# A graph network on one Trainium2 core: the order of a square's small transfers, its store and its subtractions

## The chip, the cores and the metric

The kernel runs on one core of a Trainium2 chip. The metric is the device time of one execution in microseconds (us), as a median over runs. Three runs of the kernel before took 11475.05, 11484.36 and 11488.69 us.

A core has a matrix engine (PE), a vector engine (DVE), a scalar engine for activations (ACT), a general one (POOL) and a queue that here only issues transfers (SP). Each works through its own instructions in order, and they wait for one another by semaphores. Transfers between DRAM and the on-chip memory are issued by SP or POOL and carried out by 16 DMA engines.

## The reference

Four layers on a graph of N = 3327 nodes with 128 features and a dense 3327 x 3327 matrix `adj`. Only the first layer matters here: attention with D = 128 heads of H = 8 elements, in which `adj` is added twice to the scores.

```python
q = (x @ Wq.T).reshape(d, n, h)
k = (x @ Wk.T).reshape(d, n, h)
v = (x @ Wv.T).reshape(d, n, h)
a = jnp.einsum('dnh,dmh->dnm', q, k) * scale
a = a + spatial_encoding + edge_encoding      # both are adj
a = jax.nn.softmax(a, axis=2)
out = jnp.einsum('dnm,dmh->dnh', a, v)
out = out.reshape(n, h * d)
return out @ Wo.T
```

The other three layers multiply features by `adj` or its transpose and come after the attention.

## The kernel before, in words

The kernel computes transposed scores: for a chunk `c` of 476 queries (7 chunks), a group `g` of 4 heads (32 groups) and a pair `q` of key tiles (13 pairs), so 7 x 32 x 13 = 2912 pairs. The sum starts in a PSUM bank with the transposed `adj` tile (`seed`, L660, on DVE), PE adds the products of keys and queries (`scores`, L666), ACT takes the exponential (`exps`, L678 and L681; in three pairs of a group a part of it is done on DVE by a polynomial, L692 to L703), and PE sums values with it (`values`, L719). At a group's end DVE copies the sums (`OS`, L727) and POOL sends them out in four transfers (L731).

The order is written by hand. The loop at L790 goes through slots, four to a pair, and everything is emitted in that order; each engine keeps it. What a pair emits besides its own work is:

- `loads` (L733): at the second pair of each group SP issues the next group's load: 16 transfers of keys (`KT`, L564), 24 of queries (`QS`, L566 and L568) and one of values (`VR`, L581), 41 in all. At the fifth pair POOL negates queries (L576), lays out values (`VA`, L586) and with a small copy (`seen`, L590) waits for all of them; PE's first product of the next group waits for `seen`.
- whatever `plan` has put down for the pair (L803 to L805), emitted ahead of that pair's `loads`.

`plan_squares` (L761) plans the squares. A square is a strip of 128 rows of `adj` which has to be transposed into columns (`cols`, 128 partitions x 26 tiles x 128) for the next chunk, and from which a bound for each row's scores must be subtracted so that the exponential stays in range. The first 4 of the 26 squares are done before the attention; the other 22 are spread over chunks 0 to 5, each starting in group 7k + 1 of its chunk. A square goes through these steps:

1. Four quarters, one in each of four groups: `load` (SP), `turn` (two transposes on DVE) and `largest` (a row maximum on DVE, L297, into `rm`). The last `largest` comes one pair before the pair called U below.
2. `store` (L300, SP): 1664 KB from `cols` to `adjT`, in pieces of 512 bytes. The later layers read it, and chunk 0 and a bit of chunk 1.
3. `gather` (L312, SP): four transfers of 512 bytes each from `rm` to `rowmax_d` in DRAM, element by element: 4 x 128 writes of four bytes.
4. `back` (L317, SP): `four`, the same maxima read again with the rows on the partitions.
5. `finish` (DVE, L321 and L322, then SP, L323): the maximum of the four, plus a bound of the products, and its write to `bound_d`, 128 writes of four bytes.
6. `spread` (L304, SP): the bounds read to all partitions (`on_all`), 64 KB. SP has to wait for the landing of `bound_d` before it issues this.
7. `shift` (L307, POOL): 13 subtractions of `on_all` from two tiles of `cols` each, in place. They need `on_all`, and the store from `cols` must be over.
8. `store` again, to `adjS`, which the next chunk's loads (L604) read in its predecessor's last group.

`cols`, `rows` and `on_all` have one buffer each, so the next square's first transpose waits for the store to `adjS`.

Of the kernel before, what the change touches and what calls it, by code (L numbers as in the profile page):

```python
# [29 lines left out]
NQ = NT // 2  # L30
# [55 lines left out]
def squares_of(c):  # L86

    return 0 if c < 0 else -(-min(CW * (c + 1), NP) // P)
# [3 lines left out]
def gnn_kernel(ctx: ExitStack, tc: tile.TileContext, x, adj, Wq, Wk, Wv, Wo, embed, layer,  # L92
# [12 lines left out]
    shifted_by_tile = adjS.rearrange("(p t) n -> t p n", t=NT)  # L105
# [233 lines left out]
    with tc.tile_pool(name="a1", bufs=1) as a1, tc.tile_pool(name="a2", bufs=2) as a2, \  # L339
# [23 lines left out]
        for t0 in range(0, NT, 2):  # L363
            for s in "kq":
# [3 lines left out]
                for i in range(2):  # L368
                    t = t0 + i
                    sq = a4.tile([P, H, P], F32, name="sq")  # L370
# [167 lines left out]
    with tc.tile_pool(name="e1", bufs=1) as e1, tc.tile_pool(name="e_adj", bufs=30) as e_adj, \  # L538
# [76 lines left out]
        with tc.If(loose < 1), tc.manual_schedule():  # L615
# [117 lines left out]
            def loads(u):  # L733

                c, g, q = pairs[u]
                k = c * NG + g
                if k + 1 < NC * NG:
                    nxt = divmod(k + 1, NG)
                    if q == 1:
                        load_qk(*nxt)  # L740
                        v_of[k + 1] = load_v(*nxt)
                    if q == 4:
                        negate_q(*nxt)
                        spread_v(*nxt, v_of.pop(k + 1))
                        here[k + 1] = all_here(*nxt)
                if c + 1 < NC and (g, q) == (0, 0):
                    plan_squares(c)
                if g == NG - 1 and c + 1 < NC:
                    if q == 0:
                        shift_of[c + 1] = load_shift(c + 1)  # L750
                        adj_of[c + 1] = []
                    while len(adj_of[c + 1]) < min(NT, 2 * q + 6):
                        adj_of[c + 1].append(load_adj(c + 1, len(adj_of[c + 1]), shift_of[c + 1]))
# [4 lines left out]
            def plan(u, f, *a):  # L758
                behind.setdefault(u, []).append((f, a))

            def plan_squares(c):  # L761
                for k, s in enumerate(range(squares_of(c), squares_of(c + 1))):
                    sq, u = Square(e_t, s), (c * NG + 7 * k + 1) * NQ
                    for j in range(4):
                        plan(u, sq.load, j)
                        plan(u + 7, sq.turn, j, 0)
                        plan(u + 11, sq.turn, j, 1)
                        plan(u + 12, sq.largest, j)
                        u += NQ
                    for k, f in ((0, sq.store), (0, sq.gather), (3, sq.back), (7, sq.finish), (10, sq.spread)):  # L770
                        plan(u + k, f)
                    for k in range(NQ):
                        plan(u + NQ + k, sq.shift, 2 * k, 2 * k + 2)
                    plan(u + 2 * NQ + 1, sq.store, shifted_by_tile)

            v0 = load_v(0, 0)
            load_qk(0, 0)
# [6 lines left out]
            def in_slot(i):  # L784

                j = -i % 4
                return (i - 3 * j) // 4, j


            for i in range(-4, 4 * n + 15):  # L790
                u, j = in_slot(i)
# [16 lines left out]
                u = (i - 14) // 4  # L808
# [4 lines left out]
                if at % 2:  # L813
                    for k in (1, 2):
                        u, j = in_slot(i + k)
                        if 0 <= u < n:
                            scores(u, j)
                    u, r = ((i - 11) // 4, 0) if at == 3 else ((i - 13) // 4, 1)
# [114 lines left out]
    def arr(name, w=D):  # L933
        return big.tile([P, NT, w], F32, name=name)
# [121 lines left out]
    with tc.tile_pool(name="g1", bufs=1) as g1:  # L1056
# [19 lines left out]
        f = sm.div(sm.artanh(yn, L1_MAX_TANH), yn)  # L1076
# [33 lines left out]
    with tc.tile_pool(name="h1", bufs=1) as h1:  # L1110
# [14 lines left out]
        f = sm.mul(sm.div(sm.artanh(pn, L2_MAX_TANH), pn), pf)  # L1125
# [8 lines left out]
        u, rr = arr("y"), sm.new()  # L1134
# [88 lines left out]
```

## Time and profile before

| | us |
|---|---|
| median of three runs | 11484.36 |
| the profiled execution | 11474.29 |
| its span | 11472.2 |
| of it the attention loop, about 440 to 10510 | 10070 |
| ACT busy in the attention loop | 9812 |
| PE busy in the attention loop | 9828 |
| DVE busy in the attention loop | 7682 |
| POOL busy in the attention loop | 1845 |
| mean share of the DMA engines busy in the attention loop | 0.52 |

The profile is that of one execution. Its lines name an engine, a source line, an operation and the tiles: `four<-rowmax_d` is a transfer or an instruction that reads `rowmax_d` and writes `four`. In a list of waits the numbers are the total in us, the number of times and the longest one; `DVE b L321 <- DMA four<-rowmax_d` means that DVE stood idle ahead of its instruction on L321 until that transfer had landed. In a timeline the numbers ahead of the engine are the start and the length in us, and `x4` counts merged instructions; `SPq` is SP's queue, whose lengths are those of the issue and not of the transfer. A busy matrix engine is not necessarily at its peak, as the ends of its instructions are modelled.

Other rows that touch the change, from the page and the waits of the whole span:

| what | count | us |
|---|---|---|
| subtractions `cols<-cols,on_all` on POOL, median length | 286 | 0.745 |
| POOL's wait for `on_all` ahead of them | 22 | 259.8 |
| wait of SP for the transposes ahead of the first store (L300) | 25 | 323.0 |
| wait of SP for the subtractions ahead of the second store (L300) | 22 | 238.0 |
| POOL's wait for queries ahead of a negation (L576) | 336 | 775.4 |
| POOL's wait for values ahead of their layout (L586) | 162 | 689.8 |

### The profile page before, as it was taken

The page shows a single profiled execution, that of the slowest core. Times are in us where ns is not written, and L with a number is a line of the kernel's source. Part 1 is how long each engine was busy: PE and PEld are TensorE (multiplying, and loading weights), DVE is VectorE, ACT ScalarE, POOL GpSimd, SP SyncE. Part 2 cuts the span into 40 slices and gives each one's busy share as a digit, 9 for nine tenths or more (in the row PEclk, how much of TensorE's full clock was granted, in tenths as well). Part 3 has the DMA queues.
Part 4 walks back from the last instruction along what each step waited for, and adds up shares of the span by engine and source line. Part 5 has one row for each costly group of instructions (what it writes and reads, how often), then busy time and mean ns, then how long its engine had stood idle before and what let it go on. Part 6 is the DMA issues. An engine that isn't in the chain of part 4 may idle for free.

```text
span 11472.2 us, 205583 instructions
## 1 busy us (share of the span) xinstructions
PE 10797.5 (94%) x72980; PEld 3664.2 (32%) x72980; DVE 8332.8 (73%) x13563; ACT 10115.1 (88%) x13718; POOL 2045.1 (18%) x3417
## 2 busy tenths in 40 slices
PE   4599999999999999999999999999999999998779
PEld 2133333333333333333333333333333333334444
DVE  5577777777777777777777777777777777777633
ACT  3599999999999999999999999999999999996220
POOL 5211111211112111111111121111111111111000
PEclk8799999999999999999999999999999999999889
DMA  8755555555555554555555555555554544444447
GB/s 243 247 94 97 98 90 113 98 93 97 93 109 99 98 92 86 104 99 97 93 93 111 97 98 90 95 115 93 96 92 85 108 79 85 82 81 126 155 174 272
DMA packets 732443, 1280.87 MB, mean 112 GB/s; under 512 B 190462, under 2 KB 607750, under 8 KB 714908
## 3 DMA queue, kind: packets, MB, share of 16 engines
q1 hardware_dynamic: 689528, 1138.10, 49.6%
q0 software_dynamic: 41888, 129.51, 3.8%
q8 instruction: 591, 9.68, 0.4%
q14 instruction: 436, 3.57, 0.1%
HBM read 1082.90 MB, written 184.09 MB: 110 GB/s over the span
## 4 chain that ended last, share of the span: by engine, by line
ACT 45%; PE 35%; issue 7%; DMA 5%; DVE 3%; SPq 1%; POOL 0%; POOLq 0%; DVEq 0%; ACTq 0%
ACT e L678 38%; PE po L719 16%; PE S L666 13%; ACT e L681 7%; PE pu L1016 5%; DMA QS<-qS_d 2%; DMA KT<-kS_d 1%; DVE S L660 1%; DMA four<-rowmax_d 1%; DVE e L701 0%; SPq L564 0%; PE pu L968 0%; DMA rowmax_d<-rm 0%; DVE OS L727 0%; DMA ot<-oT_d 0%
## 5 line engine op out<-in xcount | busy, mean ns | idle before, releaser
L678 ACT ACTIVATE e<-S 128x952 f32<-128x952 f32 (+1 forms) x9408 | 8749.2, 1176 | 204.2 <-PE S L666 203.1
L719 PE MATMUL po<-e,VA 128*9 128x476 f32 (+1 forms) x46592 | 5761.3, 567 | 19.4 <-DVE OS L727 1.4
L660 DVE COPY S<-a 128x476 f32<-128x476 f32 (+1 forms) x5824 | 3815.4, 655 | 1980.3 <-ACT e L678 1508.8
L666 PE MATMUL S<-QS,KT 64*128 64x476 f32 (+1 forms) x23296 | 4866.0, 451 | 228.9 <-DVE S L660 222.2
L666 PEld LDWEIGHTS S<-QS,KT 64*128 64x128 f32 x23296 | 2435.2, 184 | 5365.6 <-issue 1652.4
L681 ACT ACTIVATE e<-S 128x476 f32<-128x476 f32 (+1 forms) x3808 | 2421.2, 785 | 37.6 <-PE S L666 37.4
L701 DVE SCALAR_TENSOR_TENSOR e<-e,h 128x476 f32<-128x476 f32 (+1 forms) x2016 | 1375.1, 682 | 46.1
L731 POOL DMA_DIRECT2D oT_d<-OS x896 | 473.6, 534 | 4639.3 <-DVE OS L727 4555.5
L719 PEld LDWEIGHTS po<-e,VA 128*9 128x9 f32 x46592 | 691.1, 88 | 1585.3 <-issue 1493.4
L576 POOL TENSOR_SCALAR QS<-QS 32x476 fp32r<-32x476 f32 (+1 forms) x1344 | 851.8, 634 | 1446.2 <-DMA QS<-qS_d 775.4
L692 DVE TENSOR_SCALAR h<-S 128x476 f32<-128x476 f32 (+1 forms) x672 | 438.8, 653 | 78.5 <-PE S L666 7.1
L701 DVE SCALAR_TENSOR_TENSOR e<-h 128x476 f32<-128x476 f32 (+1 forms) x672 | 452.0, 673 | 0.0
L696 DVE TENSOR_TENSOR h<-h,h 128x476 f32<-128x476 f32 (+1 forms) x672 | 442.9, 659 | 0.0
L703 DVE SCALAR_TENSOR_TENSOR e<-e,h 128x476 f32<-128x476 f32 (+1 forms) x672 | 439.8, 654 | 0.0
L134 ACT COPY uT<-pu 128x494 f32<-128x494 f32 (+1 forms) x12 | 6.6, 547 | 426.3 <-PE pu L1016 426.3
L586 POOL COPY VA<-VR 128x832 f32<-128x832 f32 x224 | 199.9, 892 | 950.8 <-DMA VR<-v_d 689.8
L1016 PE MATMUL pu<-strip,h 128*128 128x494 f32 (+2 forms) x728 | 294.1, 565 | 38.9 <-ACT h L949 38.9
L694 DVE TENSOR_SCALAR h<-h 128x476 f32<-128x476 f32 (+1 forms) x672 | 313.1, 466 | 23.2
L1016 PE MATMUL pu<-strip,y 128*128 128x494 f32 (+2 forms) x728 | 294.5, 567 | 28.7 <-DVE y L1003 17.6
L698 DVE TENSOR_SCALAR h<-h 128x476 int32<-128x476 f32 (+1 forms) x672 | 286.7, 427 | 22.9
L307 POOL TENSOR_TENSOR cols<-cols,on_all 128x256 f32<-128x256 f32 x286 | 236.4, 859 | 260.0 <-DMA on_all<-bound_d 259.8
L293 DVE STREAM_TRANSPOSE cols<-rows 128x416 f32<-128x416 f32 x208 | 203.7, 984 | 21.3 <-DMA rows<-in_adj_dram 13.5
(186 smaller groups left out, 2456.7 us busy)
## 6 DMA issues: line engine op xcount, KB each, us to landing
KT<-kS_d SPq DMA_DIRECT2D x1792, 208.0 KB
KT<-kS_d SPq DMA_DIRECT2D x1792, 104.0 KB
VR<-v_d SPq DMA_DIRECT2D x224, 416.0 KB
strip<-adjT POOLq DMA_DIRECT2D x39, 1663.5 KB, 8.0
strip<-adjT SPq DMA_DIRECT2D x36, 1663.5 KB
QS<-qS_d SPq DMA_DIRECT2D x3072, 14.9 KB
QS<-qS_d SPq DMA_DIRECT2D x1536, 29.8 KB
adjT<-cols SPq DMA_DIRECT2D x26, 1664.0 KB
```

The source lines that it names most:

```text
L576: nc.gpsimd.tensor_scalar(QS[b][r0:r0 + 32, j + 1, :w], QS[b][r0:r0 + 32, j, :w].bitcast(F32), -1.0, 0.0, op0=ALU.mult, op1=ALU.add)
L660: touch(u, [r], nc.vector.tensor_copy(bank(u, r), adj_of[c][2 * q + r][:, :w]))
L666: x = nc.tensor.matmul(bank(u, r), KT[b][64 * r:64 * r + 64, max(0, j - 1), q * P:(q + 1) * P], QS[b][64 * r:64 * r + 64, j, :w], start=Fa ...
L678: touch(u, (0, 1), nc.scalar.activation(e[:, :, :w], S[:, odd:even + 1, :w], AF.Exp, scale=2.0))
L681: touch(u, [r], nc.scalar.activation(e[:, 1 - r, :w], bank(u, r), AF.Exp, scale=2.0))
L692: touch(u, [1], nc.vector.tensor_scalar(f, bank(u, 1), LOG2_E2, EXP_LEAST, op0=ALU.mult, op1=ALU.max))
L696: nc.vector.tensor_tensor(f, f, whole, op=ALU.subtract)
L701: nc.vector.scalar_tensor_tensor(e, f if k == 4 else e, EXP_C[k], f, op0=ALU.add, op1=ALU.mult)
L703: nc.vector.scalar_tensor_tensor(e, e, EXP_C[0], power.bitcast(F32), op0=ALU.add, op1=ALU.mult)
L719: nc.tensor.matmul(po[32 * j:32 * j + H + 1, :w], VA[k % 2][:, 2 * pairs[v][2] + of, j, :], e_of[v, j][:, 1 - of, :w], start=(q == 0 and r ...
L731: nc.gpsimd.dma_start(oT_d[:, d * N + c * CW:d * N + c * CW + w], o[32 * j:32 * j + H + 1, :w])
L1016: nc.tensor.matmul(pu[c][:, :w], y[:m, t, :], s[:m, c * AW:c * AW + w], start=(t == 0), stop=(t == NT - 1))
```

## The change

Only `plan_squares` is touched.

```diff
-                    for k, f in ((0, sq.store), (0, sq.gather), (3, sq.back), (7, sq.finish), (10, sq.spread)):
+                    for k, f in ((0, sq.gather), (3, sq.back), (7, sq.finish), (8, sq.store), (10, sq.spread)):
                         plan(u + k, f)
                     for k in range(NQ):
-                        plan(u + NQ + k, sq.shift, 2 * k, 2 * k + 2)
-                    plan(u + 2 * NQ + 1, sq.store, shifted_by_tile)
+                        plan(u + NQ + 5 + k, sq.shift, 2 * k, 2 * k + 2)
+                    plan(u + 2 * NQ + 6, sq.store, shifted_by_tile)
```

With U the pair after the last quarter's (the first pair of a group), the gathers stay at U and the store to `adjT` goes from ahead of them to U + 8, behind `finish` and ahead of `spread`. The 13 subtractions go from U + 13 .. U + 25 to U + 18 .. U + 30, and the store to `adjS` from U + 27 to U + 32. On SP the next group's load (emitted at U + 1) is then directly behind the four gathers; the store to `adjT` stands between the write of `bound_d` and the read of `on_all`; the store to `adjS` stands behind the load emitted at U + 27 instead of ahead of it. On POOL eleven subtractions stand behind the negations, the layout of values and `seen` of the pair U + 17, and two between the sending of results and the negations of U + 30, where before three stood ahead of the results of the group before, two behind them and eight behind that group's `seen`. PE, DVE and ACT keep their order.

## The prediction

> **What bounds the kernel now.** I read the page first, then the waits of all engines, the chain of one short window, the timeline of SP's queue in it, and SP's waits.
>
> ```profile
> span 11472.2 us, 205583 instructions
> ...
> PE 10797.5 (94%) x72980; PEld 3664.2 (32%) x72980; DVE 8332.8 (73%) x13563; ACT 10115.1 (88%) x13718; POOL 2045.1 (18%) x3417
> ...
> ACT 45%; PE 35%; issue 7%; DMA 5%; DVE 3%; SPq 1%; POOL 0%; POOLq 0%; DVEq 0%; ACTq 0%
> ```
>
> The attention loop lies between 440 and 10510 us; there ACT is busy 9812 of 10070 us (windows), so ACT sets the pace, and a change outside ACT is worth only what it gives of ACT's 258 idle us. The waits say where most of these are:
>
> ```profile
> DVE b L321 <- DMA four<-rowmax_d: 208.4, 22, 10.7
> ACT e L678 <- PE S L666: 203.1, 63, 9.6
> ```
>
> Twenty-two squares are turned beside the attention. In each, DVE stops at the reduction of `four` (L321) for 208.4 / 22 = 9.47 us, and ACT idles nearly as long, since the seeds of the banks (L660) queue behind it. The issues of results on POOL (L731) show the price: groups begin theirs at 4171.09, 4214.91, 4269.35 and 4313.38, so 43.8, 54.4 and 44.0 us apart; the square's group is 10.4 us long. The square of that group, in SP's queue:
>
> ```profile
> 4199.05 0.53 SPq L300 DMA_DIRECT2D adjT<-cols  x1
> 4202.00 4.19 SPq L312 DMA_DIRECT2D rowmax_d<-rm  x4
> 4206.29 0.82 SPq L564 DMA_DIRECT2D KT<-kS_d  x2
> 4207.17 0.41 SPq L566 DMA_DIRECT2D QS<-qS_d  x1
> 4210.83 1.36 SPq L568 DMA_DIRECT2D QS<-qS_d  x2
> ...
> 4235.13 0.39 SPq L581 DMA_DIRECT2D VR<-v_d  x1
> 4235.57 0.51 SPq L317 DMA_DIRECT2D four<-rowmax_d  x1
> 4239.59 0.34 SPq L323 DMA_DIRECT2D bound_d<-b  x1
> 4247.04 0.34 SPq L304 DMA_DIRECT2D on_all<-bound_d  x1
> 4257.21 0.80 SPq L564 DMA_DIRECT2D KT<-kS_d  x2
> ```
>
> The read of `four` comes behind a group's whole load (KT, QS, VR: 41 transfers), so it is late because the load ends late. Here the load takes 28.8 us from first to last issue. The next but one group, with the other store (`adjS`) 8.9 us ahead of its load, takes 23.2:
>
> ```profile
> 4292.35 0.53 SPq L300 DMA_DIRECT2D adjS<-cols  x1
> 4301.24 0.79 SPq L564 DMA_DIRECT2D KT<-kS_d  x2
> ...
> 4324.40 0.40 SPq L581 DMA_DIRECT2D VR<-v_d  x1
> ```
>
> So what delays the square's load? The chains and SP's waits:
>
> ```profile
> 4199.05 11.76 DMA adjT<-cols
> ...
> 4235.57 3.13 DMA four<-rowmax_d
> ```
>
> ```profile
> 1313.68 9.92 DMA rowmax_d<-rm
> ```
>
> ```profile
> SPq L304 <- DMA bound_d<-b: 148.7, 22, 7.2
> SPq L568 <- DMA adjT<-cols: 61.1, 22, 4.4
> SPq L568 <- DMA rowmax_d<-rm: 18.0, 17, 2.3
> ```
>
> SP's issue at 4210.83 is released by the store's landing (4199.05 + 11.76); counted from the store, it is the ninth transfer (store, four gathers, two KT, one QS before it). So eight are in flight and the ninth waits for the first; the later ones then wait for the gathers. A gather lands 9.9 us after its issue. And `bound_d`, 128 four-byte writes with nothing around them, needs 4247.04 - 4239.59 = 7.4 us: small writes to DRAM are slow by themselves.
>
> **What the Trainium skill says.** In "DMA: Bandwidth & Descriptors", "Specifications", transfers under 512 B miss the line rate and are read-modify-writes. In "Anatomy of one DMA — SWDGE (gpsimd) path" it puts a fixed cost of about 2 us on a DMA, mostly the write receipt, heaviest for HBM. The trace agrees in kind, not in size: 7.4 us for `bound_d`, against 3.13 for the read of `four` into SBUF. "Queues, rings and completion order" says that a completion mark lands only after every earlier write of its DMA engine. The trace fits: the load behind the gathers starts slowly, and the store behind which they were issued is marked landed only after 11.76 us.
>
> **The change, part by part.** Call the first gather's issue T0 (4202.00). It is released by the last `largest` on DVE and does not move: the store in front was issued 2.95 us before it.
>
> Removed ahead of the load: the store (1664 KB). The gathers' issues cost 4.19 us with the store in front; a QS issue beside them 0.41, so four cost about 1.8 (estimate). First KT: T0 + 4.3 becomes T0 + 1.9. PE frees KT in time: in the next two groups the first KT goes out 12.1 us before the results' issue (4257.21 to 4269.35), here 8.6, so it is ready at about T0 + 0.8.
>
> The gathers stay in front of the load. Their landing is the unknown, bounded from both sides. By `bound_d`, the first lands at T0 + 7.4 and the fourth, issued at T0 + 1.4, at T0 + 8.7; now they land at T0 + 9.9 and, with the last issued at T0 + 3.7 and some 7 us under way like `bound_d`, at about T0 + 10.7. That is 2.0 to 2.5 us sooner. If small writes were slow only for the store before them, the load would start at T0 + 1.9 like an ordinary one, some 6.4 us sooner; if four gathers take four times the room of one, nothing is gained. I take `bound_d`, since it is the same kind of write in an empty queue, and its upper end, since the ninth transfer waits for the first gather: 2.4. To this comes one place more in the flight of eight, as the store no longer holds one: a transfer is 24 / 41 = 0.6 us of the load, and I take 0.4. Sum 2.8 us sooner for VR, `four` and the end of DVE's stop.
>
> In the shown square DVE arrives at T0 + 26.5 and `four` at T0 + 36.7; after, T0 + 33.9. Mean stop: 9.47 - 2.8 = 6.7 us. Over 22 squares 22 x 2.8 = 61.6 us, at one to one, because ACT's 203.1 idle us answer to DVE's 208.4. Next late is the same thing: `four` behind the load.
>
> Moved: the store to pair 8, on SP after `bound_d`'s issue and before `on_all`'s. SP has nothing between these but the wait for `bound_d` (148.7 / 22 = 6.8 us), which hides the 0.5 us issue. `on_all` runs behind the store, which goes at T0 + 35.3; a strip of its size lands in 8.0 us (the page's DMA issues), so by T0 + 44. `on_all`, now asked for at T0 + 45.0 and used 4.4 later (POOL's 4251.41), is asked for at T0 + 42.2 and comes by T0 + 49. No load is held: the next starts at T0 + 52 (55.2 now, less 2.8). Cost nothing; if that cover were gone, that load has 15 us of room to the next group.
>
> Moved: the 13 subtractions, 5 pairs later (16.9 us at 43.8 / 13 = 3.37 each), behind the next group's negations, VA copy and `seen` on POOL: eleven run together when these are done, two after the next results' issue and ahead of the next negations. Two cost 1.44 us (POOL's timeline); POOL then waits for QS anyway. The wait for `on_all` (11.7 us of POOL per square) goes, and was worth nothing: POOL is 18% busy.
>
> Moved: the second store from ahead of a load to after it, and about 28 us later (T0 + 118 instead of T0 + 90.4). It moves nothing on the path: that load was not slower (23.2).
>
> Sum on the profiled execution: 11474.3 (span 11472.2 and 2.1 around it) - 61.6 = 11412.7. The median of the runs is 10.1 above that execution; carried over, 11423.
>
> **Rivals.**
> A, the forecast: small writes stay in front. 11423; with 1.5 to 4.5 us a square, 11385 to 11451.
> B, the store is the whole delay. The load takes an ordinary 24 us from T0 + 1.9; `four` lands 3.5 later, at T0 + 29.4; stop 2.9, saving 6.5 x 22 = 143: 11341. For it: the slow start of the load and the store's 11.76 us end together. Against: `bound_d`'s 7.4 us without any store.
> C, the gathers take all that the store gave: they go out together and land near T0 + 10 as before. Under 1 us a square: 11473. For it: they are 512 single writes on the same few rows, `bound_d` only 128. Against: the four now land within a us of each other, behind a store.
> D, slower: the second store lands too late, and the next square's transposes, in order on DVE, wait for `cols` as L321 does now. The store goes at T0 + 118 and lands some 8 to 12 later; the first transpose comes at pair 46, T0 + 164. It decides only past 34 us of room. Sixteen squares have a successor in their chunk; 9 us beyond the room would cost 144, less the 62: 11566. Against it: the room.
> That the change does not do what it says is out: the order of SP's instructions shows it so.
>
> **How the numbers follow.** A 0.68, B 0.13, C 0.14, D 0.05. A measurement here can tell about 0.2%, 23 us, from no change. A and B are faster; C is mostly no change, with a fifth of it beyond 23 us; D slower. Faster 0.84, same 0.11, slower 0.05. The range 11370 to 11476 holds A with the scatter of single runs (14 us) and most of C; left out are B and D, 0.18.
>
> **What would show it.** First KT about 2 us behind the first gather; VR's issue at T0 + 30 (33 now); DVE's stop at L321 about 6.7 x 22 = 148 us in all, and ACT's wait on L666 falling by the same; groups of 51.5 us at the squares, 43.8 elsewhere. Wrong if the stop falls under 80 us (B) or stays over 185 (C), or if `cols` transposes wait for `adjS` (D).

## The result, and the profile after

| | before | changed |
|---|---|---|
| median of 6 runs, us | 11483.54 | 11438.33 |
| lowest to highest | 11475.05 to 11488.69 | 11435.56 to 11449.45 |
| ratio, 95% interval | | 0.9962 (0.995 to 0.9975) |
| the profiled execution, us | 11474.29 | 11439.36 |

The changed kernel is 45 us faster by the medians and 35 us by the two profiled executions. The forecast was 11423 us. The head of the changed kernel's page comes first, and below it the two waits on which the prediction was built:

```profile
span 11437.2 us, 205561 instructions
...
PE 10803.1 (94%) x72980; PEld 3659.9 (32%) x72980; DVE 8338.7 (73%) x13563; ACT 10117.7 (88%) x13718; POOL 2054.9 (18%) x3417
...
ACT 42%; PE 37%; issue 7%; DMA 5%; DVE 4%; SPq 1%; POOL 0%; DVEq 0%; POOLq 0%; ACTq 0%
```

```profile
ACT e L678 <- PE S L666: 170.2, 84, 7.9
DVE b L321 <- DMA four<-rowmax_d: 154.6, 22, 8.3
```

ACT is as busy as before. DVE's stop for `four` is 154.6 / 22 = 7.03 us a square instead of 9.47. It has become shorter and has not gone. ACT's wait for L666 fell too, but by 32.9 us in all where DVE's stop fell by 53.8. SP's queue at the same square as in the prediction (its first gather is now at 4189.22):

```profile
4189.22 1.75 SPq L312 DMA_DIRECT2D rowmax_d<-rm  x4
4191.08 0.83 SPq L564 DMA_DIRECT2D KT<-kS_d  x2
4191.96 0.42 SPq L566 DMA_DIRECT2D QS<-qS_d  x1
4192.42 4.98 SPq L568 DMA_DIRECT2D QS<-qS_d  x2
...
4220.33 0.39 SPq L581 DMA_DIRECT2D VR<-v_d  x1
4220.76 0.51 SPq L317 DMA_DIRECT2D four<-rowmax_d  x1
4224.84 0.34 SPq L323 DMA_DIRECT2D bound_d<-b  x1
4225.23 0.53 SPq L300 DMA_DIRECT2D adjT<-cols  x1
4232.24 2.64 SPq L304 DMA_DIRECT2D on_all<-bound_d  x1
4242.49 0.80 SPq L564 DMA_DIRECT2D KT<-kS_d  x2
```

The four gathers take 1.75 us to issue instead of 4.19, and KT follows 1.86 us after the first of them. But the two QS issues that come as eighth and ninth transfer take 4.98 us: SP stands there until the first gather has landed. Over all squares SP's waits show the same; this line stood at 18.0 us before, and its neighbour, the wait for the store `adjT<-cols`, is no longer in the list:

```profile
SPq L568 <- DMA rowmax_d<-rm: 58.0, 19, 4.5
```

The load still takes 29.3 us.

How the 35 us come about is read from the issues of a group's results on POOL, and of the subtractions between them, in the changed kernel's timeline:

```profile
4158.32 2.10 POOL L731 DMA_DIRECT2D oT_d<-OS  x4 [12.65 <-DVE OS L727]
4202.11 1.08 POOL L731 DMA_DIRECT2D oT_d<-OS  x2 [24.96 <-DVE OS L727]
...
4254.64 2.09 POOL L731 DMA_DIRECT2D oT_d<-OS  x4 [29.71 <-DVE OS L727]
4271.03 10.24 POOL L307 TENSOR_TENSOR cols<-cols,on_all 128x256 f32<-128x256 f32 x11
4298.91 2.26 POOL L731 DMA_DIRECT2D oT_d<-OS  x4 [17.64 <-DVE OS L727]
```

These are 43.8, 52.5 and 44.3 us. From the copies of the results on DVE (L727), over all 22 squares:

| mean length of a group, us | before | changed |
|---|---|---|
| with a square's end (U) | 54.21 | 52.16 |
| the one behind it | 44.05 | 44.52 |
| the second behind it | 43.82 | 43.81 |

22 x 2.05 = 45.1 us are won at the square's end and 22 x 0.47 = 10.3 us are lost in the group behind it. About 4 us more go in one group, the one ahead of the last square's end, which takes 52.5 us instead of 48.4; PE waits there 6.2 us for the next keys (`seen`), and waited 2.9 before. From the first results of the attention to the last it is 30.5 us in all. The remaining 4.4 of the profiled 34.9 us lie ahead of and behind the attention, where the two kernels do the same and where the profiled executions of this document differ by up to 5.9 us anyway. The first number is the prediction's mechanism, the two losses were not in its sum.

### The profile page after: what moved, and what is told of

Its sections match the earlier page's. It is cut to its first block, busy times and chain, and to the rows that moved or that the text cites. A ratio compares the mean times of both kernels' runs of the same rounds, so it can differ in the third digit from the quotient of the medians.

```text
span 11437.2 us, 205561 instructions
## 1 busy us (share of the span) xinstructions
PE 10803.1 (94%) x72980; PEld 3659.9 (32%) x72980; DVE 8338.7 (73%) x13563; ACT 10117.7 (88%) x13718; POOL 2054.9 (18%) x3417
## 4 chain that ended last, share of the span: by engine, by line
ACT 42%; PE 37%; issue 7%; DMA 5%; DVE 4%; SPq 1%; POOL 0%; DVEq 0%; POOLq 0%; ACTq 0%
ACT e L678 35%; PE po L719 17%; PE S L666 14%; ACT e L681 7%; PE pu L1016 5%; DMA QS<-qS_d 2%; DMA KT<-kS_d 2%; DVE S L660 1%; DVE e L701 1%; DMA four<-rowmax_d 1%; PE pu L968 0%; SPq L564 0%; DVE OS L727 0%; DMA ot<-oT_d 0%; DVE xs L1003 0%
## 5 line engine op out<-in xcount | busy, mean ns | idle before, releaser
L660 DVE COPY S<-a 128x476 f32<-128x476 f32 (+1 forms) x5824 | 3814.1, 655 | 1994.3 <-ACT e L678 1521.1
L666 PE MATMUL S<-QS,KT 64*128 64x476 f32 (+1 forms) x23296 | 4869.7, 452 | 188.9 <-DVE S L660 178.3
L666 PEld LDWEIGHTS S<-QS,KT 64*128 64x128 f32 x23296 | 2435.1, 184 | 5333.6 <-issue 1642.7
L701 DVE SCALAR_TENSOR_TENSOR e<-e,h 128x476 f32<-128x476 f32 (+1 forms) x2016 | 1395.6, 692 | 46.1
L701 DVE SCALAR_TENSOR_TENSOR e<-h 128x476 f32<-128x476 f32 (+1 forms) x672 | 451.5, 672 | 0.0
L696 DVE TENSOR_TENSOR h<-h,h 128x476 f32<-128x476 f32 (+1 forms) x672 | 440.4, 655 | 0.0
L698 DVE TENSOR_SCALAR h<-h 128x476 int32<-128x476 f32 (+1 forms) x672 | 288.1, 429 | 22.9
```

The costliest lines, as they stand in the source:

```text
L660: touch(u, [r], nc.vector.tensor_copy(bank(u, r), adj_of[c][2 * q + r][:, :w]))
L666: x = nc.tensor.matmul(bank(u, r), KT[b][64 * r:64 * r + 64, max(0, j - 1), q * P:(q + 1) * P], QS[b][64 * r:64 * r + 64, j, :w], start=Fa ...
L696: nc.vector.tensor_tensor(f, f, whole, op=ALU.subtract)
L701: nc.vector.scalar_tensor_tensor(e, f if k == 4 else e, EXP_C[k], f, op0=ALU.add, op1=ALU.mult)
```

## The experiments

The theory at this point: the gathers' small writes hold up the load in front of which they stand, `four` waits for the load, DVE waits for `four`, and a square costs what DVE stops there; and the subtractions, now eleven in one piece, stretch DVE's instructions. Nine kernels took this apart. All times are medians beside runs of the kernel before on the same chip. These were at 11478.5 us for the two halves and for the kernels with the gathers alone or nothing ahead of the load, at 11473.1 for the kernel without subtractions, and at 11479.0 for the other four; the changed kernel's ratio puts it at about 11435, 11430 and 11435 there.

**The two halves of the change.** The first keeps the new order of gathers and store, with the subtractions and the second store where they were:

```diff
-                        plan(u + NQ + 5 + k, sq.shift, 2 * k, 2 * k + 2)
-                    plan(u + 2 * NQ + 6, sq.store, shifted_by_tile)
+                        plan(u + NQ + k, sq.shift, 2 * k, 2 * k + 2)
+                    plan(u + 2 * NQ + 1, sq.store, shifted_by_tile)
```

> The new order of gathers and store, but the subtractions and the second store where they were before (pairs U+13 to U+25, store at U+27). Theory: the changed kernel loses about 0.5 us in each of the 22 groups behind a square because POOL now makes eleven subtractions in one piece beside DVE's two-operand instructions; so this one is about 10 us faster than the changed kernel (near 11428), its L701 on DVE back near 682 ns in the mean, DVE's stop at L321 unchanged at about 154 us. Rival: the place of the subtractions costs nothing, and the 0.5 us a group come from the store at pair 8; then it is at 11438 with the group behind a square still 44.5 us.

Measured: 11420.66 us, ratio 0.9951 (0.9937 to 0.9965); 14 us less than the changed kernel's share. The intervals of the two ratios overlap, so it is the trace that decides: the group behind a square is back at 44.15 us, DVE's stop is 153.9 us and L701 is at 683 ns.

The second has the old order of store and gathers, and the late subtractions.

> The other half alone: store and gathers as before the change, the subtractions and the second store five pairs later. Theory: about 10 us slower than before (near 11494), DVE's stop at L321 unchanged at 208 us, L701 near 692 ns. Rival (the place of the subtractions costs nothing): 11484 as before.

Measured: 11488.94 us over 21 runs, ratio 1.0009 (1.0003 to 1.0016); 10 us slower than before, with the group behind a square at 44.65 us, the stop at 212.5 and L701 at 691 ns. The halves, -58 and +10, make -48 against about -44 for the whole. The order is the gain and the late subtractions are a loss.

**The subtractions left out.**

```diff
-                    for k in range(NQ):
-                        plan(u + NQ + 5 + k, sq.shift, 2 * k, 2 * k + 2)
```

> The changed kernel without the 13 subtractions of each square inside the attention loop (L307; the bound is then not taken off these columns). Theory: they cost what they stretch of DVE's two-operand instructions beside them, 44 us of DVE in all, of which the group behind a square loses 0.7 us (44.5 against 43.8): that group falls to 43.8, L701 to about 675 ns in the mean, the time by some 15 us to about 11420; DVE's stop at L321 stays near 154 us. Rival: the 0.7 us come from something else in that group (the read of on_all, the results of POOL): it stays at 44.5 and the time at 11435.

Measured: 11414.84 us, ratio 0.9948 (0.9935 to 0.9962), 15 us under the changed kernel's share; the group behind a square is at 43.81 us, the stop at 154.4. So the loss is the subtractions' own; it isn't the late second store, which this kernel keeps. The mean of the DVE instruction that is most often beside them moves the way that was expected. The line is that of the page's groups, first of the changed kernel, then of this one:

```profile
L701 DVE SCALAR_TENSOR_TENSOR e<-e,h 128x476 f32<-128x476 f32 (+1 forms) x2016 | 1395.6, 692 | 46.1
```

```profile
L701 DVE SCALAR_TENSOR_TENSOR e<-e,h 128x476 f32<-128x476 f32 (+1 forms) x2016 | 1376.2, 683 | 46.1
```

The mean fell to 683 ns and not to the 675 expected. It stood at 682 before the change, with the subtractions at their old pairs; what else lengthens it was not followed up. In the timeline of the changed kernel the instructions beside the eleven subtractions (4271.03 to 4281.27) can be seen:

```profile
4273.97 0.64 DVE L696 TENSOR_TENSOR h<-h,h 128x476 f32<-128x476 f32 x1
4274.64 0.83 DVE L698 TENSOR_SCALAR h<-h 128x476 int32<-128x476 f32 x1
4275.40 1.19 DVE L701 SCALAR_TENSOR_TENSOR e<-h 128x476 f32<-128x476 f32 x1
4276.51 1.40 DVE L660 COPY S<-a 128x476 f32<-128x476 f32 x2
4277.82 2.86 DVE L701 SCALAR_TENSOR_TENSOR e<-e,h 128x476 f32<-128x476 f32 x3
```

L698 takes 0.83 us where its mean with no work of POOL beside it is 0.41, the first L701 1.19 instead of 0.65. The copies into PSUM (L660), 1.40 for two, take what they always take. L696 takes its usual 0.64 although a subtraction runs beside it; that subtraction takes 1.24 us where the median is 0.755, so of the two instructions either one can be the longer. It isn't any work on POOL that costs here, but which instructions of DVE it falls beside. That these longer instructions make up the whole 0.47 us of the group is argued from this timeline and not measured by itself.

**Where the price of a square lies.** Finish, the step in which DVE asks for `four`, goes from pair 7 to pair 10, store and spread follow it; nothing else differs from the changed kernel.

```diff
-(0, sq.gather), (3, sq.back), (7, sq.finish), (8, sq.store), (10, sq.spread)
+(0, sq.gather), (3, sq.back), (10, sq.finish), (11, sq.store), (13, sq.spread)
```

> The changed kernel with finish at pair 10 instead of 7, store at 11, spread at 13. The load stays as it is (about 28.8 us from first KT to VR). Theory: what a square costs is DVE's stop at L321 alone, so with four landing at T0+34 and DVE arriving at T0+36.6 the stop falls from 154 us to under 15 and the time to about 11438-150 = 11290. Rival: the long load costs by itself (late keys for PE, or traffic beside the engines), and a good part of the 8.3 us by which a square's group is longer stays: 11350 or more.

Measured: 11251.72 us, ratio 0.9804 (0.9789 to 0.9819). There is no stop at L321 any more, though the load still takes 28.5 us in the mean, and the square's group is at 43.84 us like any other. The gain over the changed kernel, some 183 us, is larger than the stop: 22 times the group's whole excess of 8.35 us, of which the stop is 7.03. The rest goes with it. In the square of the prediction, before the change, a second idle stretch of ACT of 1.39 us follows the first of 9.18, while PE and ACT get going again:

```profile
4241.44 0.96 ACT L678 ACTIVATE e<-S 128x952 f32<-128x952 f32 x1 [9.18 <-PE S L666]
4243.79 2.67 ACT L678 ACTIVATE e<-S 128x952 f32<-128x952 f32 x3 [1.39 <-PE S L666]
```

The granted clock is no rival for this gain. Over the attention loop it is 0.99 before and 1.00 here, and the median of all groups is 43.8 us in both.

**Gathers, store, both or neither ahead of the load**, all with finish at pair 10. Gathers behind the load, store behind finish (neither):

```diff
+(2, sq.gather), (3, sq.back), (10, sq.finish), (11, sq.store), (13, sq.spread)
```

> As the run with finish at pair 10, but the four gathers are issued behind the load (pair 2) instead of ahead of it. Theory: the gathers' small writes hold the load up; without them in front it takes the ordinary 24 us, starting at once, and the gathers land about 7 us after their issue, also without any store near them. DVE's stop under 30 us, time near 11290. Rival: the load is long because of its place beside the square's end (transposes, row maxima), not because of the gathers: it stays near 28 us and four comes at T0+40, so that the stop is about 3.5 us a square, 75 us in all, and the time 11360.

The store alone ahead, the gathers behind:

```diff
+(0, sq.store), (2, sq.gather), (3, sq.back), (10, sq.finish), (13, sq.spread)
```

> The store to adjT ahead of the load, as before the change, with the gathers behind the load and finish at pair 10. One look at the load of a square's group with the store alone in front. Theory: the store in front costs the load little, because its 512-byte writes land in some 7.5 us and are nearly over when the keys' transfers start: 24 to 25.5 us from first KT to VR, first KT as early as without a square. Rival (the store is what delays): 27 us or more. The stop at L321 stays under 10 us either way.

The kernel before with nothing but a later finish and spread (both ahead):

```diff
-(0, sq.store), (0, sq.gather), (3, sq.back), (7, sq.finish), (10, sq.spread)
+(0, sq.store), (0, sq.gather), (3, sq.back), (10, sq.finish), (13, sq.spread)
```

> The kernel before with finish at pair 10 and spread at 13, and nothing else: store, gathers, load in the old order. Theory: four lands at T0+36.1 in the mean and DVE arrives at T0+36.6, so the stop falls from 208 us to under 25, and with it the whole 10.4 us by which a square's group is longer: about 11255, nearly all that the other runs gained. Rival: with store and gathers in front the load ends too late for something else too (POOL's layout of values, the next load behind bound_d), and 50 us or more of the gain are missing.

| ahead of the load | load's length, mean us | its first KT, us after the square's last row maximum | VR, us after it | stop at L321 in all, us | time, us | ratio |
|---|---|---|---|---|---|---|
| neither | 24.3 | 0.8 | 25.2 | under 1 | 11245.87 | 0.98 (0.9785 to 0.9815) |
| store | 26.6 | 0.9 | 27.5 | 9.8 | 11265.52, one run | |
| gathers (finish at 10, the run above) | 28.5 | 2.0 | 30.5 | 0 | 11251.72 | 0.9804 (0.9789 to 0.9819) |
| both | 28.5 | 4.6 | 33.1 | 0 | 11255.04 | 0.9807 (0.9792 to 0.9822) |

So the gathers delay the end of the load by 5.3 us, and the store by 2.3 alone and 2.6 beside them. The theory had the gathers right. For the store alone its 24 to 25.5 us of load were too short and the rival's 27 too long. In SP's queue with neither ahead, one can see the gathers' landing, since the read of `four` waits for it:

```profile
4103.14 0.77 SPq L564 DMA_DIRECT2D KT<-kS_d  x2
...
4127.73 0.39 SPq L581 DMA_DIRECT2D VR<-v_d  x1
4128.22 3.29 SPq L312 DMA_DIRECT2D rowmax_d<-rm  x4
4137.26 0.38 SPq L317 DMA_DIRECT2D four<-rowmax_d  x1
```

4137.26 is 9.0 us after the first issue and 5.8 after the last ended, with no store near. And the times of the table tell the other half: with finish at pair 10 the place of the store and the gathers is worth little. The last row has the subtractions at their old pairs and the others have them late, so it is to be compared with the last experiment below (neither ahead, old pairs, 11248.11 us): 7 us. With late subtractions it is 6 us from the gathers ahead to neither. Both are near the scatter of single runs, and far from 45. (The one run with the store alone is 20 us slower than neither; its groups at and behind a square are 0.3 and 0.4 us longer. It was run once, and why was not followed up.) The old order with a late finish gets all but 7 us of what the best order gets, because its ACT hardly waits any more:

```profile
PE S L666 <- DVE S L660: 25.9, 51, 1.0
ACT e L678 <- PE S L666: 13.7, 31, 0.8
```

(These are the waits between 600 and 10510 us; the longest of ACT is 0.8 us, 9.6 before.)

**The size of the gathers' writes.** Another layout of `rowmax_d` makes a gather 32 writes of 16 bytes; reading it back takes four transfers.

```diff
-rowmax_d[i, ...].rearrange("(j x) -> x j", x=32)
+rowmax_d[i, ...].rearrange("(x j) -> x j", x=32)
-nc.sync.dma_start(self.four, rowmax_d[:, ...].rearrange("i p -> p i"))
+for j in range(4):
+    nc.sync.dma_start(self.four[32 * j:32 * j + 32, :],
+                      rowmax_d[:, self.s * P + j:(self.s + 1) * P:4].rearrange("i p -> p i"))
```

> The changed kernel with another layout of rowmax_d: a gather is 32 writes of 16 bytes instead of 128 of 4 bytes, and four is read back by four transfers instead of one. Theory: the number of small writes makes the gathers slow, so they land in some 4 us instead of 7, the load shrinks from 28.6 us towards 26, and although the reading back takes 1.3 us more on SP, the stop at L321 falls from 154 us to about 110 and the time to about 11390. Rival: the 7 us are a fixed cost of writes to DRAM; then the load stays at 28.6 us, the stop rises by 22 x 1.3 to about 183 us and the time to about 11465.

Measured: 11357.24 us, ratio 0.9895 (0.988 to 0.991), more than expected. In SP's queue (L566 and L583 are the old L564 and L581):

```profile
4157.64 1.70 SPq L312 DMA_DIRECT2D rowmax_d<-rm  x4
4159.45 0.83 SPq L566 DMA_DIRECT2D KT<-kS_d  x2
...
4184.06 0.39 SPq L583 DMA_DIRECT2D VR<-v_d  x1
4184.50 2.96 SPq L318 DMA_DIRECT2D four<-rowmax_d  x4
```

The load takes 24.6 us, 24.8 in the mean: with gathers ahead, within half a us of what it takes with none. By the semaphores in the trace a gather lands 1.6 us after its issue in the mean, where it was 7.0 in the changed kernel. That settles what in the gathers was slow: not that DRAM is written, and not the amount (512 bytes each in both), but 128 scattered writes of four bytes. What is left of the stop, 94.5 us, is the load itself, the finish at pair 7 and the 2.96 us of four reads.

**The subtractions at their old pairs with the best order.**

> The run with the gathers behind the load and finish at pair 10, with the subtractions at their old pairs (U+13 to U+25, store at U+27). Theory: no stop at L321, and fewer of DVE's two-operand instructions beside the subtractions; 5 to 10 us faster than that run, about 11238. Rival: the subtractions wait for on_all at pair 13, hold POOL ahead of the results and negations, and the keys come late: slower than 11246.

Measured: 11248.11 us, ratio 0.9799 (0.9786 to 0.9813). The theory's gain is not there, and the 2 us on the rival's side are less than single runs scatter: it is level with the same kernel with late subtractions (11245.87). The group behind a square is at 44.19 against 44.27 us, the square's own at 44.09 against 43.85. As the rival said, with finish at pair 10 `on_all` comes later, and POOL stands in front of the subtractions for 476 us in all (260 before): the old places are not the old times any more, and more of DVE's instructions fall beside them (L701 702 ns in the mean, 694 in the other). So the fastest version is a tie of the two; both are about 2% faster than the kernel before.

## Why the prediction was right, and where it was off

The way, the chain of causes and the range held. By its steps:

- That ACT sets the pace and that DVE's stop at L321 is what a square costs: right. Removing the stop alone brought the group to 43.8 us, and the whole 10.4 us by which it was longer went with the stop of 9.47.
- "One to one" for a stop that only becomes shorter: too much. ACT's wait on L666, which was to fall by the same as the stop, fell by 32.9 us for its 53.8. In the last square the stop fell by 7.6 us, to 1.05, because DVE came late, behind PE's wait for keys in the group before, and there some 4 us were lost again. In each of the other 21 the stop fell by 2.2 us and the group by 1.7; where the half us stays was not followed up.
- First KT at T0 + 1.9: measured 1.89 in the mean.
- The gathers stay slow without the store, by the measure of `bound_d`: right, 7.0 us in the mean against 7.4. This is what decided between cases A and B, and the 16-byte gathers confirm the mechanism. The line that the Trainium skill draws at 512 bytes ("DMA: Bandwidth & Descriptors", "Specifications") is not where slow and fast part here: 16 bytes are far below it too, and land in 1.6 us. The 2 us that the prediction takes from "Anatomy of one DMA — SWDGE (gpsimd) path" are given there for transfers that POOL issues; these are SP's.
- The store's 11.76 us do not follow from what the prediction cites of "Queues, rings and completion order": that speaks of earlier writes, and the store is ahead of the gathers. What the runs show is that a store with such writes beside it lands late on either side of them: 11.8 us in the mean ahead of the gathers, 13.0 behind `bound_d` at its new place, 8.3 ahead of a load with no small writes near. Why stays open. The prediction gave the new place 8.0 us; the other 5 cost nothing, since the subtractions that need the store over come later.
- VR sooner by 2.8 us: in the mean over the squares it came 32.7 us after the first gather before and 30.5 after, 2.2 sooner, and DVE began on `four` at 36.2 and 34.1. This term was too large by 0.6. The 2.4 for the gathers held: just behind them the load is 2.5 us ahead (its eleventh transfer goes out 13.1 us after the first gather before, 10.6 after). The 0.4 for a place more in the flight of eight found nothing to do: the load's fifth transfer waits for the first gather before and after. Another 0.3 was lost in the rest of the load. That the stop's total, 154.6 us, is so near the 148 named is luck: it has the last square's 7.6 us in it.
- The subtractions' new place, for which the prediction had only POOL's own time: this term was wrong. They cost 0.47 us in each group behind a square, 10 us in the profiled execution, and 10 to 15 by the three runs that moved or left them out. The prediction looked at POOL's own share and at who waits for POOL; it did not ask beside which DVE instructions they would now run.
- The wait for `on_all` gone and worth nothing, the stores' new places free: right. DVE's transposes show no wait for `adjS`, so case D's room was there.

The sum therefore: 61.6 us predicted for the profiled execution, 45.1 at the squares' ends, less 10.3 behind them and 4 ahead of the last; 34.9 measured with what lies outside the attention. By the medians 45.2 us are measured. That this is nearer to 61.6 is no merit of the sum: the profiled execution before was quicker than all six timed runs, the one after was not.

What the prediction missed altogether is the larger lever beside the change: not when `four` arrives, but that DVE asks for it at pair 7. With finish at pair 10 the order that the change corrects hardly matters.

## What to carry to other kernels

When an engine on the path stops for a result, first see whether it can ask for it later, if what hangs on the result has room for that: three pairs' delay of one small instruction was worth 224 us here, the better order of the transfers 58. A small transfer written ahead of a large load isn't small if it is made of single elements: count its writes, and give it a layout with longer runs before moving anything. Work moved on an engine that is far from busy can still cost, by what it runs beside.

## What was not expected of the hardware

- 128 four-byte writes to DRAM land 7.0 us after their issue, 32 writes of 16 bytes of the same 512 bytes 1.6 us. Whether it is their number, their size or the order of their addresses is not separated here.
- Beside POOL's subtractions (128x256, two operands in on-chip memory) DVE's instructions that neither read nor write PSUM took up to twice as long (L698 0.83 for 0.41 us, L701 1.19 for 0.65), or the subtraction did instead (1.24 for 0.755); copies into PSUM took none longer (0.65 either way).
- A store of 1664 KB landed 11.8 to 13.0 us after its issue with transfers of four-byte writes just behind or just ahead of it, and 8.3 us with none near.
